# Row turns on VectorE, weight splits on ScalarE and an early gated shared expert in an adaLN block with a mixture of experts

## The chip, the core and the metric

The kernel runs on one core of a Trainium2 chip. Five engines work side by side, each through its own instructions in order: TensorE (PE; PEld is its weight load), VectorE (DVE), ScalarE (ACT), GpSimd (POOL) and SyncE (SP), which here issues nearly all DMAs. An instruction that waits holds up everything behind it on its engine. Sixteen DMA engines move the data. The metric is the device time of one execution in microseconds (us); lower is better.

## What is computed

Input x has 32 batches of 256 tokens with 128 features. The reference, cut to what matters:

```python
h = _layernorm(x) * (1 + ca) + sa
x = x + ga * _L0_attn_ref(h, ...)            # 16 heads, causal, softmax over queries
h = _layernorm(x) * (1 + cb) + sb
x = x + gb * _L0_ffn_ref(h, ...)
# the feed-forward part, for each token:
scores = sigmoid(logits);  sc = scores + gate_bias
# 2 of 4 groups of 8 experts by the sum of their two best sc; of those 16 experts the best 6
routed = einsum('te,teh->th', cw, silu(x @ w_gate) * (x @ w_up) @ w_down)
shared = silu(x @ shared_w_gate) * (x @ shared_w_up) @ shared_w_down
anchor = einsum('tl,tlh->th', acw, ao)       # one of 16 anchor experts, by the best expert
out = routed + shared + 0.1 * anchor
```

`gb` is a gate for each batch and feature. All data is 32-bit.

## The kernel before

**Attention stage** (0 to about 860 us). Tokens go in 16 chunks of 512 (`CH`), each in 8 steps of two heads. Beside the products, portions of work for other chunks (norms, routing) are dealt out by a table of steps and places. `through_dram` (L399) turns a normalized chunk: it is stored to DRAM and read back by `load_blocks` (L388) in 32x32 blocks, which DVE transposes. The turned chunk c stays in `h2_all[c]`, the residual in `x1_all[c]`. Routing writes each token's row (128 features and 52 numbers: for each of the 4 groups 8 expert weights, 4 anchor weights and the place of its result) by indirect DMA to DRAM (`rows_d`), sorted by group, twice for each token. `route_write` (L837) lays out the expert weights, even experts of a group ahead of odd ones.

**Expert stage.** 35 lists (tiles) of up to 512 rows of one group each. For tile j there are five units k: four of 128 of the group's 512 hidden columns (two experts each) and one of 128 anchor columns. A unit is, on PE, `up` (L1237): pg and pu, each a 128x128 by 128x512 product; and `down` (L1250) of the unit before: four products into py. Between them ACT makes Silu of pg (L1245) and DVE multiplies by pu (L1246) and by `bt` (L1247), the routing weights spread over the hidden columns' partitions.

The order is written out by hand. In unit 0 of tile j, SP gets `fetch_rows(j+3)` (L1159: two values loaded from a table, then one DMA of 360 KB) and `fetch_weights(j+2)` (L1175: four DMAs); in unit 1 DVE picks the tile's own group out of the rows' numbers (`weights_mine(j+2)`); in unit 2 `weights_turn(j+2)` (L1204) turns them on PE (pc), copies them by ACT (cwt), stores them to DRAM (cd) and at once reads them back spread (bt, six DMAs); in unit 3 `rows_turn(j+1)` (L1228) turns the rows by four PE transposes (ph) and an ACT copy (h). After a tile, `send` (L1273) copies py by ACT (y) and POOL writes it to `y_d` by four indirect DMAs, each row to its token's place.

**Shared expert.** For pairs n of chunks, seven ahead of the tiles and the last among them: `shared_up` (L1292) and, one step later, `shared_down` (L1305), whose result takes the place of `h2_all[c]`, copied by ACT for one chunk and by DVE for the other. The two PSUM banks that it uses in the opening are single, so the next `shared_down` waits for those copies. Emitted ahead of all this on SP are `fetch_rows` of tiles 0 to 2 and `fetch_weights` of tiles 0 and 1 (L1371 to L1374).

**The output pass.** When a chunk's tokens are complete (from tile 17 on, at most one chunk a tile, in unit 4), `pass_load` (L1328) reads both results of each token and the gate; `pass_sum` (L1345), due in unit 3 of the next tile, adds them and the shared result on DVE and multiplies by the gate on POOL; `pass_out` (L1366), due in unit 1 of the tile after, adds the residual and stores. The last chunk goes through `pass_rest` (L1354) at the end.

Of the kernel before, what the change touches and what calls it, by code (L numbers as in the profile page):

```python
# [16 lines left out]
P = 128  # L17
# [39 lines left out]
def adaln_block_kernel(  # L57
# [80 lines left out]
    def late_loads():  # L138

        nc.sync.dma_start(out=wd_sb, in_=w_down.rearrange("(k p) m -> p k m", p=P))  # L140
        nc.sync.dma_start(out=ad_sb, in_=an_down.rearrange("(k p) m -> p k m", p=P))
        nc.sync.dma_start(out=sg_sb, in_=sh_gate)
        nc.sync.dma_start(out=su_sb, in_=sh_up)
        for h in range(P // SI):
            nc.sync.dma_start(out=sd_sb[h * SI : (h + 1) * SI], in_=sh_down)
# [174 lines left out]
    with ExitStack() as actx:  # L320
# [516 lines left out]
        def route_write(c):  # L837

            w, ws, one = (chunk[c].pop(k) for k in ("w", "ws", "one"))
            meta = chunk[c]["rows"][:, :, D:].rearrange("p i (g w) -> p i g w", w=GW)  # L840
            wk = w.rearrange("p i (g k q) -> p i g k q", g=NG, q=2)
            for q in range(2):
                nc.gpsimd.tensor_tensor(
                    meta[:, :, :, q * EPG // 2 : (q + 1) * EPG // 2], wk[:, :, :, :, q],
                    ws.unsqueeze(2).unsqueeze(3).to_broadcast([P, NT, NG, EPG // 2]), ALU.mult,
                )
            pair = one.rearrange("p t (g l e) -> p t g l e", g=NG, e=2)
            nc.gpsimd.tensor_tensor(
                meta[:, :, :, EPG : GW - 1], pair[:, :, :, :, 0], pair[:, :, :, :, 1], ALU.add
            )  # L850
# [298 lines left out]
        fin = actx.enter_context(tc.tile_pool(name="fin", bufs=3, reuse_waits="tile"))  # L1149
# [9 lines left out]
        def fetch_rows(j):  # L1159
            t = T[j]  # L1160
            of, n = t["of"]
            t["g_sp"] = nc.sync.value_load(of.table[0:1, 0, n : n + 1], min_val=0, max_val=NG - 1)
            r = nc.sync.value_load(of.table[0:1, 1, n : n + 1], min_val=0, max_val=NG * SPAN)
            t["rw"] = rwp.tile([P, NT, ROW], F32, tag="rw", name=f"rw_{j}")
            got = nc.sync.dma_start(
                out=t["rw"],
                in_=rows_d[bass.ds(r, CH), :].rearrange("(p i) f -> p i f", i=NT),
            )
            if j < FIRST:
                tc.declare_no_dep(  # L1170
                    got.ins, group="late rows", reason="this tile holds rows of earlier chunks"
                )
                tc.add_to_no_dep_group("first tiles", got.ins)

        def fetch_weights(j):  # L1175
            t = T[j]
            g = t.pop("g_sp")
            for key, src, srca in (("wg", w_gate, an_gate), ("wu", w_up, an_up)):
                w = wp.tile([P, KU + 1, P], F32, tag=key, name=f"{key}_{j}")
                nc.sync.dma_start(  # L1180
                    out=w[:, 0:KU, :].rearrange("p k f -> p (k f)"),
                    in_=src[:, bass.ds(g * (KU * P), KU * P)],
                )
                nc.sync.dma_start(out=w[:, KU, :], in_=srca[:, bass.ds(g * P, P)])
                t[key] = w

        def weights_mine(j):

            t = T[j]
            of, n = t["of"]  # L1190
            mm = mp.tile([P, NT, NG, GW], F32, tag="mm", name=f"mm_{j}", bufs=1)
            nc.vector.tensor_tensor(
                mm,
                t["rw"][:, :, D:].rearrange("p i (g w) -> p i g w", w=GW),
                of.mine[:, n, :].unsqueeze(1).unsqueeze(3).to_broadcast([P, NT, NG, GW]),
                ALU.mult,
            )
            m = mp.tile([P, GW, NT], F32, tag="m", name=f"m_{j}")
            nc.vector.tensor_reduce(m, mm.rearrange("p i g w -> p w i g"), AX.X, ALU.add)
            ix = mp.tile([P, NT], U32, tag="ix", name=f"iy_{j}", bufs=5)  # L1200
            nc.vector.tensor_copy(ix, m[:, GW - 1, :])
            t.update(m=m, ix=ix)

        def weights_turn(j):  # L1204
# [10 lines left out]
            bt = bcp.tile([P, KU + 1, CH], F32, tag="bt", name=f"bt_{j}")  # L1215
            for q in range(2):
                nc.sync.dma_start(
                    out=bt[q * EI : (q + 1) * EI, 0:KU, :],
                    in_=cd[q * KU : (q + 1) * KU].partition_broadcast(EI),
                )  # L1220
            for q in range(NG):
                nc.sync.dma_start(
                    out=bt[q * LI : (q + 1) * LI, KU, :],
                    in_=cd[2 * KU + q].partition_broadcast(LI),
                )
            t["bt"] = bt

        def rows_turn(j):  # L1228
            t = T[j]
            rw = t.pop("rw")  # L1230
            ph = ps_mm.tile([P, CH], F32, tag="mm", name=f"ph_{j}")
            for i in range(NT):
                nc.tensor.transpose(ph[:, i * P : (i + 1) * P], rw[:, i, 0:D], ident)  # L1233
            t["h"] = mp.tile([P, CH], F32, tag="h", name=f"h_{j}", bufs=2)
            nc.scalar.copy(t["h"], ph)  # L1235

        def up(j, k):  # L1237
# [4 lines left out]
            nc.tensor.matmul(pg, t["wg"][:, k, :], t["h"], start=True, stop=True)  # L1242
            nc.tensor.matmul(pu, t["wu"][:, k, :], t["h"], start=True, stop=True)  # L1243
# [3 lines left out]
            nc.vector.tensor_mul(a, a, t["bt"][:, k, :])  # L1247
# [42 lines left out]


        def shared_up(n):  # L1292
# [10 lines left out]
            return n, a  # L1303

        def shared_down(n, a, banks):  # L1305
# [5 lines left out]
            for i in range(NT):  # L1311
                for h in range(2):
# [6 lines left out]
                    )  # L1319
            for h, c in enumerate(cs):  # L1320
                (nc.scalar.copy, nc.vector.tensor_copy)[h](
                    h2_all[c], py[h].rearrange("p i d -> p (i d)")
                )
# [4 lines left out]
        def pass_load(c):  # L1328
            t = S_[c]
            t["s"] = [  # L1330
                xin.tile([P, NT, D], F32, tag="xt", name=f"s{k}_{c}") for k in range(2)
            ]
            for k, s in enumerate(t["s"]):
# [5 lines left out]
            t["gate"] = fin.tile([P, BPC, D], F32, tag="gate", name=f"gate_{c}")  # L1339
            nc.sync.dma_start(  # L1340
                out=t["gate"],
                in_=gate_dram[c * BPC : (c + 1) * BPC].partition_broadcast(P),
            )

        def pass_sum(c):  # L1345
            s0, s1 = S_[c]["s"]
            nc.vector.tensor_add(s0, s0, s1)
            nc.vector.tensor_add(s0, s0, h2_all[c].rearrange("p (i d) -> p i d", d=D))
            for b in range(BPC):
                nc.gpsimd.tensor_tensor(  # L1350
# [3 lines left out]
        def pass_rest(c, b):  # L1354
# [4 lines left out]
            nc.vector.tensor_add(  # L1359
                s0, s0, h2_all[c].rearrange("p (i d) -> p i d", d=D)[:, part]  # L1360
            )
# [17 lines left out]
        for n in range(PAIRS):  # L1379
# [12 lines left out]
            if n == 3:  # L1392
                weights_turn(1)
            if n == 4:
                rows_turn(0)
        shared_down(*prev, two_banks)
# [6 lines left out]
        for j in range(LISTS):  # L1403
            for k in range(KU + 1):
# [12 lines left out]
                if k == 2 and j + 2 < LISTS:  # L1417
                    weights_turn(j + 2)
                if k == 3 and j + 1 < LISTS:
                    rows_turn(j + 1)  # L1420

# [10 lines left out]
                elif len(pair) > 1:  # L1432
                    shared_down(*pair, ((ps_mm, "mm"), (ps_mm, "mm")))
                    pair = (PAIRS,)
# [3 lines left out]
                if k == 4 and started < NCH and complete[started] <= j:  # L1438
                    pass_load(started)
                    due[j + 1, 3] = lambda c=started: pass_sum(c)  # L1440
                    due[j + 2, 1] = lambda c=started: pass_out(c)
# [61 lines left out]
```

## Time and profile before

| what | value |
|---|---|
| median of 13 executions | 1420.9 us (1416.81 to 1423.55) |
| the profiled execution | 1416.6 us, its span 1414.8 us |
| granted TensorE clock, mean | 0.986 |
| attention stage, 0 to 830: PE / DVE / ACT / POOL busy | 816 / 646 / 611 / 538 us |
| 1000 to 1200: PE / DVE / ACT / POOL busy | 200 / 123 / 64 / 59 us |
| 1200 to 1300: DMA engines' share, GB/s | 0.87, 249 |
| first product of tile 0, last y copy | 894.4, 1395.25 us |

Times in the views count from the start of the span. A line of the timeline has start, duration, engine, source line, operation, output and inputs, how many instructions were merged, and in brackets the idle time before it and what ended it. "SPq" is an issue of a DMA on SP's queue, not its landing. A busy time of PE is modelled from pipelined products, so the distance between starts tells more than durations.

### The profile page before, as it was taken

Reading aid. Unit: us, or ns where it says so; the run is one execution under the profiler, and the core shown is the slowest. Engines: PE = TensorE matmul, PEld = TensorE weight load, DVE = VectorE, ACT = ScalarE, POOL = GpSimd, SP = SyncE. Lnnn points to the kernel's source line nnn. Section 1 sums busy time; section 2 is a strip of 40 time slices with the busy share of each in tenths; the row PEclk is TensorE's granted clock in tenths of the full one; section 3 lists DMA queues with packets and bytes.
Section 4 is the critical chain, followed back from the end, with each engine's and each line's share of the span. In section 5 each row is a group of like instructions: output and inputs, shape, how many; then the busy total and the mean of one; then the engine's idle time right before and its main releaser. Section 6 shows DMA issues by size and latency. Waiting matters only on the chain. (4 is left out here: it accounts for less than half of the span.)

```text
span 1414.8 us, 33682 instructions
## 1 busy us (share of the span) xinstructions
PE 1356.8 (96%) x10543; PEld 841.9 (60%) x10543; DVE 1016.2 (72%) x4277; ACT 797.3 (56%) x2767; POOL 762.1 (54%) x1294
## 2 busy tenths in 40 slices
PE   7999999999999999999999997889999999999994
PEld 2566666666666666566666663555666666656662
DVE  5666888888878778888777775666665567766664
ACT  4777777777777777777777773322333333332331
POOL 3536467767767866767866645444232233434333
PEclk9999999999999999999999999999999999999997
DMA  4773622022022022022122114767667777878782
GB/s 152 276 265 108 219 74 60 32 74 61 31 74 62 31 73 62 30 74 62 38 68 50 39 35 128 185 165 191 171 184 211 186 217 221 256 233 245 233 221 61
DMA packets 183599, 182.50 MB, mean 129 GB/s; under 512 B 81520, under 2 KB 142656, under 8 KB 178944
## 3 DMA queue, kind: packets, MB, share of 16 engines
q1 hardware_dynamic: 172112, 159.62, 40.8%
q0 software_dynamic: 10624, 20.21, 4.3%
q8 instruction: 86, 1.41, 0.4%
q14 instruction: 89, 0.73, 0.2%
q10 hardware_dynamic: 688, 0.53, 0.1%
HBM read 121.37 MB, written 59.70 MB: 128 GB/s over the span
## 5 line engine op out<-in xcount | busy, mean ns | idle before, releaser
L549 ACT ACTIVATE e<-e,mn 128x256 f32<-128x256 f32 (+1 forms) x1024 | 453.5, 445 | 200.6 <-DVE mn L539 158.8
L539 DVE CUSTOM_DVE_ANT_0 e<-psc,mask 128x256 f32<-128x256 f32 (+1 forms) x1024 | 306.5, 345 | 9.7 <-PE pav L586 3.3
L568 POOL TENSOR_TENSOR vs<-v,rc 128x256 f32<-128x256 f32 x256 | 151.2, 611 | 223.8 <-DVE rc L557 214.8
L1279 POOL DMA_INDIRECT y_d<-y,iy x140 | 137.7, 984 | 239.9 <-ACT y L1276 207.7
L518 PEld LDWEIGHTS psc<-q,k 64*128 64x128 f32 x2048 | 166.2, 187 | 113.4 <-issue 101.6
L1246 DVE TENSOR_TENSOR a<-a,pu 128x512 f32<-128x512 f32 x175 | 120.0, 686 | 153.9 <-PE pu L1243 107.3
L1245 ACT ACTIVATE a<-pg 128x512 f32<-128x512 f32 x175 | 104.4, 597 | 178.1 <-PE pg L1242 123.4
L518 PE MATMUL psc<-q,k 64*128 64x256 f32 (+1 forms) x2048 | 202.1, 336 | 0.0
L586 PE MATMUL pav<-e,vs 128*64 128x256 f32 (+1 forms) x2048 | 194.7, 332 | 6.1 <-POOL vs L568 6.1
L549 ACT ACTIVATION_READ_ACCUMULATOR e<-e,mn 128x1 f32 x1024 | 192.4, 188 | 0.0
L1268 PEld LDWEIGHTS py<-wd_sb,a 128*128 128x128 f32 x1120 | 146.5, 191 | 71.9 <-issue 54.3
L1242 PE MATMUL pg<-h,wg 128*128 128x512 f32 x350 | 181.7, 601 | 1.4 <-ACT h L1235 1.4
L1243 PE MATMUL pu<-h,wu 128*128 128x512 f32 x350 | 180.0, 596 | 0.0
L468 PEld LDWEIGHTS po<-wo_sb,z 128*64 128x64 f32 x2048 | 120.4, 137 | 70.3 <-issue 69.6
L586 PEld LDWEIGHTS pav<-e,vs 128*64 128x64 f32 x2048 | 126.8, 136 | 58.8 <-POOL vs L568 6.7
L479 DVE TENSOR_TENSOR v<-pv,bv_sb 128x512 f32<-128x512 f32 x128 | 88.3, 690 | 92.8 <-PE pv L468 63.8
L1268 PE MATMUL py<-wd_sb,a 128*128 x1120 | 148.1, 275 | 2.9 <-issue 1.5
L856 POOL DMA_INDIRECT rows_d<-rows,ix x128 | 129.9, 1015 | 37.4 <-issue 34.6
L489 DVE TENSOR_SCALAR q<-pq,negbq 128x512 f32<-128x512 f32 x128 | 95.9, 749 | 64.2 <-PE pq L468 62.5
L468 PE MATMUL pv<-wqkv_sb,n_t 128*64 128x512 f32 x512 | 132.8, 598 | 2.3 <-DVE q L489 1.6
L468 PE MATMUL pq<-n_t,wqkv_sb 128*64 128x512 f32 x512 | 133.5, 600 | 0.7 <-ACT n_t L302 0.7
L468 PE MATMUL po<-wo_sb,z 128*64 128x128 f32 x2048 | 133.6, 273 | 0.0
(239 smaller groups left out, 1771.6 us busy)
## 6 DMA issues: line engine op xcount, KB each, us to landing
bt<-cd SPq DMA_DIRECT2D x70, 512.0 KB
rows_d<-blank SPq DMA_DIRECT2D x69, 360.0 KB
rw<-rows_d SPq DMA_DIRECT2D x35, 360.0 KB
wg<-in_w_gate_dram SPq DMA_DIRECT2D x35, 256.0 KB
wu<-in_w_up_dram SPq DMA_DIRECT2D x35, 256.0 KB
bt<-cd SPq DMA_DIRECT2D x140, 64.0 KB
s<-y_d SPq DMA_DIRECT2D x32, 256.0 KB
mb<-mod_dram SPq DMA_DIRECT2D x31, 256.0 KB
```

The lines of the kernel that those rows point to most:

```text
L468: nc.tensor.matmul(ps[r], a[:, r], b, start=start, stop=stop)
L518: nc.tensor.matmul(pb[h][:, cols], k[r, o + kb * P : o + (kb + 1) * P], q[r, o + kb * P : o + S], start=True, stop=True,)
L539: nc.vector.tensor_tensor_reduce(e[:, cols], ps[:, cols], mask[:, cols], 1.0, 3e38, ALU.add, ALU.min, mn[:, b, kb, h : h + 1],)
L549: nc.scalar.activation(e[:, cols], e[:, cols], AF.Exp, bias=mn[:, b, kb, h : h + 1], scale=-1.0, accum_out=sm[:, b, kb, h : h + 1],)
L568: nc.gpsimd.tensor_tensor(vs[:, 2 * b : 2 * b + 2], vt[:, 2 * b : 2 * b + 2, col : col + P].rearrange("p k (h d) -> p k h d", h=2), rc[:, ...
L586: nc.tensor.matmul(pav[h * DH : (h + 1) * DH, o + kb * P : o + S], vs[:, 2 * b + kb, h, :], e[:, 0 : 2 * P] if kb == 0 else e[:, 2 * P : 3 ...
L856: sent = nc.gpsimd.indirect_dma_start(out=rows_d[:, :], out_offset=bass.IndirectOffsetOnAxis(ap=ix[:, k, i : i + 1], axis=0), in_=rows[:, ...
L1242: nc.tensor.matmul(pg, t["wg"][:, k, :], t["h"], start=True, stop=True)
L1243: nc.tensor.matmul(pu, t["wu"][:, k, :], t["h"], start=True, stop=True)
L1246: nc.vector.tensor_mul(a, a, pu)
L1268: nc.tensor.matmul(t["py"][:, i, :], a[:, i * P : (i + 1) * P], w, start=k == 0 and i == 0, stop=k == KU and i == NT - 1,)
L1279: sent = nc.gpsimd.indirect_dma_start(out=y_d[:, :], out_offset=bass.IndirectOffsetOnAxis(ap=ix[:, i : i + 1], axis=0), in_=y[:, i, :], in ...
```

## The change

1. Rows. `fetch_rows` loads the 52 numbers (`rw`) and the features (`rh`) apart; the features come in 32x32 blocks by four DMAs of `load_blocks`, and `rows_turn` becomes one DVE transpose. The four PE transposes and the ACT copy go.
2. Hidden columns. Unit k now takes every fourth hidden column of the group from k on, so that partition p belongs to expert p // 16 in all four units: `bt` has two planes in place of five and takes one DMA of 256 KB for the experts (and four for the anchors, as before). `w_down` is loaded in that order. The gate and up weights arrive in their old order (`raw`) and ACT copies them to the new one: `split_weights(j+1)`, wg in unit 2, wu in unit 3, behind what was there. `route_write` needs one POOL product in place of two.
3. The spread of the weights is a function of its own, `weights_spread`, called in unit 4, two units behind the store.
4. Shared expert. `shared_up` also loads the gates of both chunks. `shared_down` multiplies by them on DVE (four products a pair, no copies) and POOL adds the result to the residual.
5. Output pass. `pass_sum` is one sum, due in unit 0 of the second tile after the load; the gate is multiplied on DVE in unit 2 (`pass_gate`), the residual added in unit 4. `pass_rest` loses a sum. The tiles of the pass come from pools of their own (6 for s, 5 for gates).

```diff
@@ late_loads
-        nc.sync.dma_start(out=wd_sb, in_=w_down.rearrange("(k p) m -> p k m", p=P))
+        nc.sync.dma_start(
+            out=wd_sb.rearrange("p (g k) m -> p g k m", g=NG),
+            in_=w_down.rearrange("(g p k) m -> p g k m", g=NG, p=P),
+        )
@@ fetch_rows
-            t["rw"] = rwp.tile([P, NT, ROW], F32, tag="rw", name=f"rw_{j}")
...
+            t["rw"] = rwp.tile([P, NT, ROW - D], F32, tag="rw", name=f"rw_{j}")
+            t["rh"] = rwp.tile([P, CH // BLK, BLK], F32, tag="rh", name=f"rh_{j}")
+            rows = rows_d[bass.ds(r, CH), :]
+            got = [
+                nc.sync.dma_start(
+                    out=t["rw"], in_=rows[:, D:].rearrange("(i p) f -> p i f", p=P)
+                ),
+                *load_blocks(t["rh"], rows),
+            ]
@@ fetch_weights
-                w = wp.tile([P, KU + 1, P], F32, tag=key, name=f"{key}_{j}")
+                raw = wp.tile([P, P, KU], F32, tag=f"{key}r", name=f"{key}r_{j}")
...
+        def split_weights(j, key):
+
+            t = T[j]
+            raw, a = t[key]
+            w = wp.tile([P, KU, P], F32, tag=key, name=f"{key}_{j}", bufs=2)
+            nc.scalar.copy(w, raw.rearrange("p f k -> p k f"))
+            t[key] = [w[:, k, :] for k in range(KU)] + [a]
@@ weights_turn
-            bt = bcp.tile([P, KU + 1, CH], F32, tag="bt", name=f"bt_{j}")
-            for q in range(2):
-                nc.sync.dma_start(
-                    out=bt[q * EI : (q + 1) * EI, 0:KU, :],
-                    in_=cd[q * KU : (q + 1) * KU].partition_broadcast(EI),
-                )
...
+        def weights_spread(j):
+
+            t = T[j]
+            cd = t.pop("cd")
+            bt = bcp.tile([P, 2, CH], F32, tag="bt", name=f"bt_{j}")
+            nc.sync.dma_start(
+                out=bt[:, 0, :], in_=cd[0:EPG].unsqueeze(1).to_broadcast([EPG, P // EPG, CH])
+            )
...
@@ rows_turn
-            ph = ps_mm.tile([P, CH], F32, tag="mm", name=f"ph_{j}")
-            for i in range(NT):
-                nc.tensor.transpose(ph[:, i * P : (i + 1) * P], rw[:, i, 0:D], ident)
...
-            nc.scalar.copy(t["h"], ph)
+            nc.vector.transpose(t["h"], t.pop("rh").rearrange("p x r -> p (x r)"))
@@ shared_up, shared_down
-            return n, a
+            return n, a, [load_gate(c) for c in cs]
...
-                (nc.scalar.copy, nc.vector.tensor_copy)[h](
-                    h2_all[c], py[h].rearrange("p i d -> p (i d)")
-                )
+                o = h2_all[c].rearrange("p (i d) -> p i d", d=D)
+                for b in range(BPC):
+                    nc.vector.tensor_tensor(
+                        tokens(o)[:, b], tokens(py[h])[:, b], by_batch(gates[h])[:, b], ALU.mult
+                    )
+                nc.gpsimd.tensor_tensor(x1_all[c], x1_all[c], o, ALU.add)
@@ the opening: pairs n
                 weights_turn(1)
+                weights_spread(0)
             if n == 4:
+                weights_spread(1)
                 rows_turn(0)
+            if n == 5:
+                split_weights(0, "wg")
+                split_weights(0, "wu")
@@ the tiles
+                if k in (2, 3) and j + 1 < LISTS:
+                    split_weights(j + 1, ("wg", "wu")[k - 2])
                 if k == 3 and j + 1 < LISTS:
                     rows_turn(j + 1)
+                if k == 4 and j + 2 < LISTS:
+                    weights_spread(j + 2)
...
                     pass_load(started)
-                    due[j + 1, 3] = lambda c=started: pass_sum(c)
-                    due[j + 2, 1] = lambda c=started: pass_out(c)
+                    due[j + 2, 0] = lambda c=started: pass_sum(c)
+                    due[j + 2, 2] = lambda c=started: pass_gate(c)
+                    due[j + 2, 4] = lambda c=started: pass_out(c)
```

## The prediction

> **What bounds the kernel now.** I read the page's busy line first, then busy time by stage, then PE's timeline in one tile of the expert stage, then SP's.
>
> ```profile
> PE 1356.8 (96%) x10543; PEld 841.9 (60%) x10543; DVE 1016.2 (72%) x4277; ACT 797.3 (56%) x2767; POOL 762.1 (54%) x1294
> ```
>
> PE is the engine to follow. The change leaves the attention stage (0 to 860) almost alone, so its worth is read from the opening of the expert stage (862 to 894, the shared expert), the 35 tiles (894 to 1395) and the tail. One tile on PE:
>
> ```profile
> 1134.51 1.05 PE L1268 MATMUL py<-wd_sb,a 128*128 x8
> 1135.40 1.02 PE L1242 MATMUL pg<-h,wg 128*128 128x512 f32 x2
> ...
> 1139.84 1.05 PE L1268 MATMUL py<-wd_sb,a 128*128 x8
> 1140.73 0.60 PE L1233 MATMUL ph<-ident,rw 128*128 128x128 f32 x4
> 1141.17 1.02 PE L1242 MATMUL pg<-h,wg 128*128 128x512 f32 x2
> ```
>
> No idle time stands on these rows. From py to the next pg it is 0.89 us (1134.51 to 1135.40), and with the four row turns between 1.33 (1139.84 to 1141.17): the turns cost PE 0.44 a tile. A unit is 2.61 (pg 0.87, pu 0.85, py 0.89), a tile 5 x 2.61 + 0.11 (pc) + 0.44 = 13.60; the y copies (L1276) indeed start 13.60 apart from 1024 to 1242. Tiles 1 to 7 need 13.5 us more than that in all, tiles after 1242 some 5.2 more. SP's queue shows the late loss:
>
> ```profile
> 1281.66 0.42 SPq L1214 DMA_DIRECT2D cd<-cwt  x1
> 1285.08 1.27 SPq L1217 DMA_DIRECT2D bt<-cd  x2
> 1286.72 1.72 SPq L1222 DMA_DIRECT2D bt<-cd  x4
> ...
> 1293.63 0.35 SPq L1165 DMA_DIRECT2D rw<-rows_d  x1
> ...
> 1296.78 0.45 SPq L1214 DMA_DIRECT2D cd<-cwt  x1
> ```
>
> Once output chunks are also loaded and stored, SP needs 14.4 us a tile (cd to cd: 13.4 to 15.4 from 1167 on), more than PE's 13.6. It falls behind about 0.8 a tile until the s loads come too late for pass_sum (L1347: 9.9 us of waiting for them). The opening:
>
> ```profile
> 866.49 6.17 SPq L1165 DMA_DIRECT2D rw<-rows_d  x3
> 872.73 0.66 SPq L1180 DMA_DIRECT2D wg<-in_w_gate_dram  x1
> ...
> 878.84 0.37 SPq L1214 DMA_DIRECT2D cd<-cwt  x1
> ```
>
> ```profile
> 875.51 0.68 DVE L1321 COPY h<-sy 128x512 f32<-128x512 f32 x1
> ```
>
> ```profile
> 875.50:885.00 9.50, 8.80 (x56) 4.13 (x58) 9.12 (x38) 3.13 (x7) 1.21 (x2) 0.82 0.63 181
> 885.00:894.40 9.40, 8.73 (x91) 5.25 (x87) 8.32 (x39) 3.68 (x8) 6.61 (x21) 1.00 0.76 167
> ```
>
> In the windows the columns are PE, PEld, DVE, ACT, POOL. DVE is busy 17.4 of 18.9 us there: the opening is bound by DVE and PE together, and DVE starts on shared results at 875.5, while SP is still issuing loads until 878.8.
>
> **The change part by part.** The sum is made against the profiled execution: 1414.8 span, 1416.6 with what lies around it. The median of 13 runs is 1420.9, 4.3 above that one.
>
> *Turns from PE to DVE.* PE loses 0.44 in 34 tiles: **-15.0**. DVE gains one 128x512 transpose, 0.70 (rows L456 and L652). In a unit DVE has two products of 0.69 (1.38 of 2.61), and extras now go one to a unit: sum 0.69, mine 1.20, gate 2 x 0.40 to 0.43, turn 0.70, out 0.68. The fullest unit is 2.58 of 2.61, and a product is done 0.5 us before PE loads it (1133.59 against 1134.09), so I cost them at nothing; with that cover gone each late one would cost its excess over 0.5. ACT loses the h copy (0.585).
>
> *Splits by ACT.* Two copies of 128x512 a tile. No row shows ACT reading at a stride. Bounds: 0.585 (L1235, contiguous) and 1.4 times that, 0.82, from DVE's strided reduce against its contiguous product of the same 208 columns (L1199 513 ns, L1192 368). I take 0.6, since a copy is nearest to a copy. ACT sits idle 2.0 us a unit, so mostly this costs nothing. But in unit 2 a split queues behind cwt, which waits for PE's pc, and Silu of the next unit waits behind both. In 23 tiles cwt starts within 1.1 us of pc, in 12 it starts 1.6 to 3.1 after. There Silu would come 1.2 late (1.4 with 0.82), of which 0.27 is hidden behind pu and 0.5 by the slack above: 0.5 to 0.7 for each of up to 12. Between 0 and 8.6 I take **+3**. The Trainium skill ("SBUF — State Buffer", Door 1: The DMA port swizzle) says SBUF has 16-byte lines and every access that crosses to a new line pays; here each element is 16 bytes from the last. By that rule the splits would stand at the slow end, the term would be 8.6 and the time 1431.6; no row here shows it on ACT.
>
> *Row loads and bt.* One 360 KB load of rows becomes one of 208-byte pieces and four of 128-byte pieces; bt falls from two of 512 KB to one of 256 KB. The same block loads (hb, 236.8 to 242) kept the 16 DMA engines 49% busy for 5.2 us, 512 packets of hd among them: about 2 us for 2048 small packets. Against that, 768 KB of bt go, 3.4 us at the 220 GB/s that bt moved at 1143 to 1146. DMA (share 0.87 at 1200 to 1300) gets lighter.
>
> On SP, each row load is about 0.55 (four hb in 1.96, plus 0.07 for the address): +2.2 a tile, less 0.6 for a bt.
>
> *Spread two units later.* Between the cd store (unit 2) and the spread (unit 4) nothing else is queued on SP. In the tiles SP still waits at bt for cd to land (70.9 us over 32 waits, 2.2 each): I cost this at **0**.
>
> *Late stage.* SP's cycle: 14.4 + 2.2 - 0.6 - 1.5 (waits of rw, weights and gate for slow bt loads, 20 us in all over the stage) = 14.5, against 13.16 on PE. It falls behind 1.3 a chunk tile instead of 0.8. pass_sum now comes two units later, so the s loads may be 11.3 late instead of 6.4: 8.5 chunk tiles instead of 7.5. So the late loss stays near what it was, 5 chunk tiles x 1.3 = 6.5 against 5.2: **+1** (-5 to +8).
>
> *Opening.* The gates of the first pair are emitted behind three row fetches and two weight fetches. SP leaves those at 878.8; twelve more loads of 0.55 make 885.4, and 2 us landing (cd to bt: 2.1) 887.4, against 875.5 for DVE's first copy. That is 12; 8 if SP is spared the slow stretch 868 to 874 (some 4 us). I take **+11**. Every instruction behind that gate on DVE waits, and PE for its banks. Then DVE has 7 x (4 x 0.396, L628, - 0.689, L1321) + 0.7 = **+7**. POOL gets 14 sums of 128x512, 1.4 each (twice 0.72, L1350), in front of chunk 15's normalization; its rows leave later, SP waits for them at hb, and the gates of the last pair are behind hb: **+3** (0 to 6). In return tile 0's own loss goes (2.9 us at 904 waiting for that same hb, 1.5 of half clock behind it; 15.5 is the bare path): **-4**, of which a new cold start takes its part. Opening: **+17** (10 to 24).
>
> *Tail.* pass_rest loses two sums of 0.424: **-0.9**. POOL's gates there go too, but the last s load waits for y_d to land.
>
> Sum: -15.0 + 3 + 1 + 17 - 0.9 = **+5.1**: 1421.7 for the profiled execution, **1426** on the scale of the median.
>
> **Rivals.**
> 1. *The opening's delay is absorbed (faster).* Tiles 1 to 7 lose 13.5 us while chunk 15 is routed and the last pair is run: PE waits for counts (1.7 at 940), for h from ACT (1.0 at 975), for a late cwt at 923. Of it PE's own work is 4.6 (pl, pr, sg, su, sy, by their rows); if the other 8.9 are waits for things that a later start meets ready, they go: 1426 - 8.9 = **1417**. It decides from 8 us absorbed (5.1 + 2.8). For it: h leaves ACT. Against: chunk 15's steps are dealt by unit and shift along.
> 2. *The spread does what it says (no change).* If SP were spared the 2.2 of waiting, its cycle is 12.3, below PE's, and the late loss goes: 5.1 - 1 - 5.2 = -1.1, **1420**. Against it: nothing is queued between.
> 3. *SP bounds the last stage (slower).* If rows cost 0.7 each and the waits stay, 15.2: 2.0 behind a chunk tile, the slack of 11.3 is gone after 5.6 of 15, the other 9 cost 2 each: 18 - 5.2 = 13 instead of 1: **1438**.
>
> **Chances.** Forecast 0.45 (1420 to 1432), rival 1 0.25, rival 2 0.12, rival 3 0.18. The range runs from rival 1 with the opening at its low end (-15 + 3 + 1 + 10 - 0.9 - 8.9 = -10.8, 1410) past rival 3 to 1442, the forecast with the opening at +24 and the splits and the late stage at their upper ends in part (7 + 5.6 + 7 = 19.6 would be 1445.6). A measurement can tell 0.2% (2.8 us) from no change. Faster 0.28 (rival 1 and the forecast's edge), within 0.12 (rival 2), slower 0.60.
>
> **What would show it.** PE: unit 2.61 and the y copies 13.16 apart in mid stage. DVE: the first gated product of the shared expert at 884 to 888 behind "DMA gate", and the first y copy near 932 (now 915.5). SP: cd to cd 14.5 in chunk tiles, bt still waiting for cd. ACT: splits of 0.6, and PE waits for DVE's product after unit 2 where cwt is late. Wrong would be: gates landing by 878, a split over 0.9 us, DVE waiting for rh.

## The result and the profile after

The changed kernel takes **1444.9 us** (median of 10; 1439.9 to 1451.7) against 1421.0 of the kernel before on the same chip: ratio **1.017** (1.0155 to 1.0184). The profiled execution has a span of 1441.7 against 1414.8, 26.9 more. The busy line of the page:

```profile
PE 1352.1 (94%) x10403; PEld 827.4 (57%) x10403; DVE 1048.8 (73%) x4349; ACT 840.7 (58%) x2794; POOL 756.9 (53%) x1264
```

PE lost its turns (140 instructions fewer), yet the span grew: its idle time did. Where, is read from four marks: the start of SP's last block loads of the attention stage (hb), the first product of tile 0, and the y copies of ACT, each a tile's end (all us, worked out from the starts in the timelines):

| stretch | before | after | difference | foretold |
|---|---|---|---|---|
| start to hb | 862.8 | 864.3 | +1.5 | 0 |
| hb to first pg | 31.6 | 55.8 | +24.2 | with the next row +17 |
| first pg to y0 | 21.1 | 20.5 | -0.6 | |
| y0 to y8 | 122.3 | 124.9 | +2.6 | the three rows of tiles -11 |
| y8 to y20 | 163.2 | 165.8 | +2.6 | |
| y20 to y34 | 194.3 | 193.4 | -0.9 | |
| y34 to the end | 19.6 | 17.1 | -2.5 | -0.9 |

The first row is no finding: over the profiled executions of all kernels here, hb lay between 858.8 and 867.8.

**The opening.** SP's and DVE's timelines of the kernel after:

```profile
868.07 0.50 SPq L1169 DMA_DIRECT2D rw<-rows_d  x1
...
883.36 0.33 SPq L1191 DMA_DIRECT2D wua<-in_an_up_dram  x1
883.73 5.27 SPq L1308 DMA_DIRECT2D gate<-gate_dram  x6
```

```profile
887.90 1.42 DVE L1347 TENSOR_TENSOR h<-sy,gate 128x256 f32<-128x256 f32 x4 [14.68 <-DMA gate<-gate_dram]
889.24 0.85 DVE L681 TENSOR_SCALAR sig<-th 128x128 f32<-128x128 f32 x1
890.01 1.77 DVE L638 TENSOR_TENSOR x<-xt,o_t 128x512 f32<-128x512 f32 x1
...
895.61 1.17 DVE L691 TENSOR_TENSOR hi<-scb 128x64 f32<-128x64 f32 x1
...
901.15 0.37 DVE L365 BATCH_NORM_AGGREGATE ln_mv<-ln_stats 128x2 f32<-128x6 f32 x4
...
901.96 1.24 DVE L701 TENSOR_TENSOR lo<-lo 128x16 f32<-128x16 f32 x1
```

The gates leave SP behind every row and weight fetch, and DVE stands 14.68 us for them. Then single operations of DVE take far longer than their neighbours: 1.17 us for one of 128x64, 1.24 for one of 128x16, where the instructions just after (L692, L702) take 0.21 and 0.17. POOL's timeline has a new operation, the sum of the shared result, beside each of them:

```profile
888.74 2.49 POOL L1350 TENSOR_TENSOR x<-x,h 128x512 f32<-128x512 f32 x2 [19.47 <-DVE h L1347]
...
894.16 2.54 POOL L1350 TENSOR_TENSOR x<-x,h 128x512 f32<-128x512 f32 x2 [1.52 <-DVE h L1347]
...
900.65 2.51 POOL L1350 TENSOR_TENSOR x<-x,h 128x512 f32<-128x512 f32 x2 [1.52 <-DVE h L1347]
```

The pairs of sums cover 888.7 to 891.2, 894.2 to 896.7 and 900.7 to 903.2, and the long DVE operations start at 889.2, 890.0, 895.6 and 902.0, all inside. Three of them end just behind a pair, whatever their own length: L638, L691 and L701 at 891.78, 896.78 and 903.20, the pairs at 891.23, 896.70 and 903.16. L365, inside the same pair as L701, takes 0.37, as it does in experiment 12 without the sums. So the long ones are held until the sum ends and not slowed in proportion; why some DVE operations are held and others not, the runs do not show. The granted clock of PE falls as well (third column from the right):

```profile
864.00:880.00 16.00, 8.86 (x76) 4.44 (x72) 2.64 (x5) 3.35 (x5) 4.06 (x5) 0.93 0.61 105
880.00:892.00 12.00, 2.70 (x16) 2.27 (x16) 4.10 (x7) 0.00 (x0) 3.10 (x3) 0.50 0.62 181
892.00:905.00 13.00, 10.74 (x56) 4.06 (x58) 12.62 (x41) 1.71 (x4) 9.17 (x10) 0.71 0.32 94
```

PE is busy 2.70 of the 12 us at 0.50. In the 13 us at 0.71 DVE is the fuller engine (12.62 against PE's 10.74). What the lower clock cost was not isolated.

**A tile.** Unit 2 of a middle tile, PE, ACT and DVE together:

```profile
1111.97 0.27 PE L1223 MATMUL pc<-ident,m 128*48 128x128 f32 x1
...
1113.68 0.26 ACT L1227 COPY cwt<-pc 48x128 f32<-48x128 f32 x1 [2.67 <-PE pg L1258]
...
1113.84 1.11 ACT L1199 COPY wg<-wgr 128x512 f32<-128x512 f32 x1
...
1114.86 0.59 ACT L1260 ACTIVATE a<-pg 128x512 f32<-128x512 f32 x1
...
1115.48 0.69 DVE L1261 TENSOR_TENSOR a<-a,pu 128x512 f32<-128x512 f32 x1 [2.72 <-ACT a L1260]
...
1116.20 0.69 DVE L1262 TENSOR_TENSOR a<-a,bt 128x512 f32<-128x512 f32 x1
...
1116.95 0.38 PE L1283 MATMUL py<-wd_sb,a 128*128 x1 [0.38 <-DVE a L1262]
```

cwt starts 1.71 after pc; the split behind it takes 1.11, not 0.6; Silu waits for it, the two products of DVE follow, and PE stands until they are done. Such a tile takes 13.8. Where cwt comes 0.35 after pc, the tiles are 13.16 apart, as foretold. In the profiled execution it is late in 23 of 35 tiles (12 before).

### The profile page after: what moved, and what is told of

Its sections match the earlier page's. It is cut to its first block, busy times and chain, and to the rows that moved or that the text cites. A ratio compares the mean times of both kernels' runs of the same rounds, so it can differ in the third digit from the quotient of the medians.

```text
span 1441.7 us, 33883 instructions
## 1 busy us (share of the span) xinstructions
PE 1352.1 (94%) x10403; PEld 827.4 (57%) x10403; DVE 1048.8 (73%) x4349; ACT 840.7 (58%) x2794; POOL 756.9 (53%) x1264
## 4 chain that ended last, share of the span: by engine, by line
PE 75%; DVE 8%; issue 5%; DMA 4%; SPq 4%; POOL 3%; ACT 1%; POOLq 0%; DVEq 0%; ACTq 0%
PE psc L521 13%; PE pav L589 12%; PE py L1283 8%; PE pv L471 8%; PE pq L471 7%; PE pk L471 7%; PE po L471 7%; PE pg L1258 7%; PE pu L1258 6%; DVE a L1261 1%; DVE a L1262 1%; SPq L395 1%; DVE e L542 1%; ACT a L1260 1%; DMA gate<-gate_dram 1%
## 5 line engine op out<-in xcount | busy, mean ns | idle before, releaser
L589 PE MATMUL pav<-e,vs 128*64 128x256 f32 (+1 forms) x2048 | 194.9, 332 | 6.1 <-POOL vs L571 6.1
L1283 PE MATMUL py<-wd_sb,a 128*128 x1120 | 151.1, 278 | 23.5 <-DVE a L1262 19.3
L1258 PE MATMUL pg<-h,wg 128*128 128x512 f32 x280 | 144.7, 599 | 0.0
L1258 PE MATMUL pu<-h,wu 128*128 128x512 f32 x280 | 143.7, 595 | 0.0
```

The lines of the kernel that those rows point to most:

```text
L589: nc.tensor.matmul(pav[h * DH : (h + 1) * DH, o + kb * P : o + S], vs[:, 2 * b + kb, h, :], e[:, 0 : 2 * P] if kb == 0 else e[:, 2 * P : 3 ...
L1258: nc.tensor.matmul(ps, t[key][k], t["h"], start=True, stop=True)
L1283: nc.tensor.matmul(t["py"][:, i, :], a[:, i * P : (i + 1) * P], w, start=k == 0 and i == 0, stop=k == KU and i == NT - 1,)
```

## The experiments

The edits are made in the changed kernel unless another is named. Ratios are to the kernel before on the same chip, with 95% intervals; the kernel after stands at 1.017. "Opening" is hb to the first pg (before 31.6, after 55.8), "middle" y8 to y20 (163.2, 165.8), "late" y20 to y34 (194.3, 193.4).

**1. e1, gates first.** The first four gates leave SP ahead of the fetches.

```diff
-            return n, a, [load_gate(c) for c in cs]
+            return n, a, [first_gates.pop(c, None) or load_gate(c) for c in cs]
...
+        first_gates = {c: load_gate(c) for c in range(4)}
         for j in range(3):
             fetch_rows(j)
```

> The gates of the first two pairs are loaded ahead of the row and weight fetches; all else is as in the changed kernel (1444.85 us). Theory (the gates wait their turn on SP): DVE's first gated product starts at about 876 instead of 887.9, 12 us go, about 1433. Rival (DVE and POOL work bounds the opening and the wait only overlaps it): tile 0's first product moves by less than 4, 1441 or more. A small loss is expected by both, since four gate loads of 0.4 us now stand ahead of the row fetches.

Measured 1429.8, ratio 1.0076 (1.0046 to 1.0106); opening 45.5. The gates' place cost 10.3 us of the opening; the theory held (DVE's first gated product starts at 872.2, earlier than foretold).

**2. e2, splits later.** `split_weights(j + 1)` in units 3 and 4, not 2 and 3: it no longer stands behind cwt.

```diff
-                if k in (2, 3) and j + 1 < LISTS:
+                if k in (3, 4) and j + 1 < LISTS:
```

> The two splits of a tile stand in units 3 and 4 instead of 2 and 3, so that no split is queued between cwt and Silu. Theory (a split of 1.12 us behind a late cwt holds back Silu): tiles are 13.16 apart from the 8th on instead of 13.80, about 20 tiles gain 0.64, 13 us, about 1432. Rival (the turn on DVE or the row loads cost the 0.64): tiles stay at 13.8, 1445. A gain smaller than 13 at 13.16 a tile would mean that SP takes over earlier in the late stage.

1432.8, ratio 1.0087 (1.0059 to 1.0115). Middle 157.9, twelve tiles of 13.16; PE's waits for DVE's product fell from 20.4 to 6.4 us in all. Held. In ten of the twelve middle tiles cwt is late as before, but now Silu follows it at once, and the tile takes 13.16 all the same:

```profile
1095.96 0.26 ACT L1227 COPY cwt<-pc 48x128 f32<-48x128 f32 x1 [2.55 <-PE pg L1258]
1096.12 0.59 ACT L1260 ACTIVATE a<-pg 128x512 f32<-128x512 f32 x1
```

**3. e3, contiguous split.** The same copy without the stride.

```diff
-            nc.scalar.copy(w, raw.rearrange("p f k -> p k f"))
+            nc.scalar.copy(w.rearrange("p k f -> p (k f)"), raw.rearrange("p f k -> p (f k)"))
```

> The splits read the weights in the order in which they lie, so the columns of gate and up weights come out in the wrong order (part of the computation is changed); places and sizes are the same. Theory (reading one element in each 16 bytes makes the copy take 1.118 us): a split takes 0.59, Silu behind a late cwt is 0.5 late beyond its slack at most, tiles are 13.2 to 13.35 apart, about 1434 to 1437. Rival (the copy is long because of its size or of what runs beside it): it stays at 1.1 and the time at 1445.

1435.8, ratio 1.0108 (1.0076 to 1.014); middle 158.9. On ACT's timeline the copy behind a late cwt now takes 0.62:

```profile
1121.68 0.26 ACT L1227 COPY cwt<-pc 48x128 f32<-48x128 f32 x1 [2.58 <-PE pg L1258]
1121.84 0.62 ACT L1199 COPY wg<-wgr 128x512 f32<-128x512 f32 x1
```

Only the order of reading differs, so the stride of 16 bytes is what makes it 1.11. Held.

**4. e4, spread at the store.** `weights_spread` back in unit 2.

```diff
                     weights_turn(j + 2)
+                    weights_spread(j + 2)
-                if k == 4 and j + 2 < LISTS:
-                    weights_spread(j + 2)
```

> The spread stands in unit 2 again, right behind the store. Theory (nothing else is queued on SP between the two, so the place makes no difference in the tiles): the same time within 2 us, 1445, with the same waits of SP for cd. Rival (the two units hide the store's landing): SP waits more for cd, its cycle grows by up to 2.2 a tile, the late stage loses 10 or more, 1455.

1439.1, ratio 1.013 (1.0106 to 1.0154): no slower than after, even 0.4% faster, where the same time was foretold. SP's waits for cd grow from 47.1 to 58.0 us, and the late stage by 1.5 (194.9); the middle is 1.4 shorter, and cwt is late in 17 tiles of the run, not 23. The later place alone gains nothing in the time.

**5. e5, turns alone.** The kernel before with only the rows' loads in blocks and their turn on DVE.

```diff
+                *load_blocks(t["rh"], rows),
...
-                nc.tensor.transpose(ph[:, i * P : (i + 1) * P], rw[:, i, 0:D], ident)
...
-            nc.scalar.copy(t["h"], ph)
+            nc.vector.transpose(t["h"], t.pop("rh").rearrange("p x r -> p (x r)"))
```

> The kernel before with one part of the change alone: rows loaded in blocks and turned on DVE. Theory (PE gains 0.44 a tile, and SP then bounds the late stage, since four more loads cost it 2.2 a tile and bt is still large): tiles 13.16 apart in mid stage, -15; in the chunk tiles SP needs 16.6 a tile, falls behind 3.4 a tile, its slack of 6.4 is gone after two, the other 13 cost up to 3.4 each instead of 5 in all: +15 to +39, together 1421 to 1445, with the y copies more than 15 apart there. Rival (SP has room): 1406, y copies 13.2 apart to the end.

1463.5, ratio 1.0299 (1.0277 to 1.0321): the direction of the SP theory, but far more than either theory gave. Tiles are 13.16 apart until the output pass begins; then they lose: middle 178.8, late 220.8, SP waits 86.9 us for cd, `pass_sum` 40.5 for its loads. Four more loads a tile beside the large bt cost far more than PE saves. That SP's issues are the limit, and not the transfers, and that the smaller bt pays for the loads in the change, is argued and not shown.

**6. e6, host order.** Gate and up weights stored in DRAM in the split order; no splits.

```diff
+        "w_gate": get("ffn_w_gate").transpose(1, 0, 2).reshape(D, NG, P, -1).transpose(0, 1, 3, 2).reshape(D, E * EI),
...
-                if k in (2, 3) and j + 1 < LISTS:
-                    split_weights(j + 1, ("wg", "wu")[k - 2])
```

> The changed kernel without its splits: the gate and up weights lie in DRAM in the order of the split columns from the start, so ACT copies nothing (an order of data outside the timed program). Theory: as with the splits in units 3 and 4, tiles of 13.16 from the 8th on until SP bounds them, 1430 to 1433. Rival (what the splits cost is mostly ACT's and DMA's time, not the wait behind cwt): clearly faster than with the splits moved, 1425 or less.

1442.9, ratio 1.0149 (1.0129 to 1.017). Missed. Middle 157.9, as without the splits' stall; but late 198.7, and in the profiled execution hb was 3.6 later than after. Why the late stage lost 5 is not settled; e18, with the tiles of after, has 197.4 there, so part of it may be scatter between executions.

**7. e7, sums later.** POOL's sums one a tile in tiles 1 to 14, not in the opening.

```diff
-                nc.gpsimd.tensor_tensor(x1_all[c], x1_all[c], o, ALU.add)
+                if n == PAIRS:
+                    nc.gpsimd.tensor_tensor(x1_all[c], x1_all[c], o, ALU.add)
...
+                if k == 3 and 1 <= j <= 2 * PAIRS:
+                    c = j - 1
+                    nc.gpsimd.tensor_tensor(
+                        x1_all[c], x1_all[c],
+                        h2_all[c].rearrange("p (i d) -> p i d", d=D), ALU.add,
+                    )
```

> POOL adds the gated shared results to the residual one chunk a tile in tiles 1 to 14 instead of in the opening. In the changed kernel's opening DVE's small products run 0.6 to 1.1 us long while POOL adds (6.0 us over what the same instructions take in the kernel before), and POOL's queue holds up chunk 15's rows. Theory (both cost the opening): tile 0's first product comes 6 to 10 us earlier, 1435 to 1439. Rival (the wait for the first gates hides them): within 3 us, 1442 or more.

1444.7, ratio 1.0161 (1.0134 to 1.0189). Missed: opening 49.3 (-6.5), but y0 to y8 128.0 (+3.1) and late 197.6 (+4.3), though no moved sum stands in the late stage. Moved, the sums gained nothing.

**8. e8, shared as before.** Shared expert as in the kernel before (copies, added in `pass_sum`, no early gates, no POOL sums); all else as after.

```diff
...
-                o = h2_all[c].rearrange("p (i d) -> p i d", d=D)
-                for b in range(BPC):
-                    nc.vector.tensor_tensor(
-                        tokens(o)[:, b], tokens(py[h])[:, b], by_batch(gates[h])[:, b], ALU.mult
-                    )
-                nc.gpsimd.tensor_tensor(x1_all[c], x1_all[c], o, ALU.add)
+                (nc.scalar.copy, nc.vector.tensor_copy)[h](
+                    h2_all[c], py[h].rearrange("p i d -> p (i d)")
+                )
...
+            nc.vector.tensor_add(s0, s0, h2_all[c].rearrange("p (i d) -> p i d", d=D))
...
```

> The changed kernel with the shared expert as in the kernel before (copies by ACT and DVE, no gates in the opening, no sums on POOL; the shared result is added in pass_sum, one sum more a chunk). Theory (the opening's 25 us are the gates, their products and the sums): the first y copy comes at 918 to 922 instead of 940.6, tiles behind it as in the changed kernel, 1421 to 1426. Rival (the row fetches on SP delay the opening by themselves): 1432 or more.

1423.4, ratio 1.0012 (0.9993 to 1.0031); opening 32.2. The time held (the first y copy came at 912.0, earlier than foretold): net, the whole loss is the shared expert's part; the rest of the change comes to nothing.

**9. e9: e8 with splits in units 3 and 4.**

> The changed kernel with the shared expert as before (copies, added in pass_sum, no early gates, no POOL sums) and the splits in units 3 and 4. My theory: what is left of the loss in the tiles is the split behind the late cwt; without it the tiles from 9 to 20, 13.8 apart with the splits in units 2 and 3, come 13.16 apart: about 12 x 0.64 = 7.7, a few more of the early ones, less what SP takes back late: 1412 (1408 to 1417). The rival, that the late stage is bound by SP alone and takes back all that the middle wins: 1420 to 1424, no change against 1423.4.

1407.6, ratio **0.993** (0.9909 to 0.995). Faster than both kernels. The theory held: by the ratio 1411 on the scale of e8, as foretold. Middle 157.9, late 193.3, where e8 has 165.8 and 196.9: the late stage took nothing back.

**10. e10: e9 with one DMA for the anchors' plane of bt.**

```diff
-            for q in range(NG):
-                nc.sync.dma_start(
-                    out=bt[q * LI : (q + 1) * LI, 1, :],
-                    in_=cd[EPG + q].partition_broadcast(LI),
-                )
+            nc.sync.dma_start(
+                out=bt[:, 1, :],
+                in_=cd[EPG : EPG + NG].unsqueeze(1).to_broadcast([NG, P // NG, CH]),
+            )
```

> The kernel of the run before, with the anchors' plane of bt spread by one DMA in place of four (the same bytes). Four issues take SP 1.80 us, one of that shape 0.68. Theory: SP's issues bound the late tiles (cd to cd 14.2 to 15.4), so 1.1 less a tile over some 12 to 15 tiles from number 20 on: about 12 less than the run before, 1400 (1396 to 1406). Rival one: the late stage is bound by the landing of the s and cd transfers, not by issues: within 2 of the run before. Rival two: one DMA of 128 partitions lands later than four of 32, bt late: slower than the run before.

1421.4, ratio 1.0026 (1.0009 to 1.0042); late 207.4. The theory failed and the second rival's forecast came: SP issues less, but the same bytes move slower. The windows some 2 to 4 us behind the spread's first issue, of e9 and then of e10 (last columns: share of the DMA engines, GB/s):

```profile
1113.00:1114.00 1.00, 1.00 (x6) 0.65 (x6) 0.96 (x2) 0.33 (x1) 0.00 (x0) 1.00 0.54 207
1114.00:1115.00 1.00, 1.00 (x4) 0.40 (x3) 0.06 (x1) 0.60 (x1) 0.00 (x0) 1.00 0.79 256
```

```profile
1123.00:1124.00 1.00, 1.00 (x6) 0.59 (x5) 0.96 (x2) 0.28 (x1) 0.00 (x0) 1.00 0.51 186
1124.00:1125.00 1.00, 1.00 (x4) 0.46 (x3) 0.00 (x0) 0.60 (x1) 0.00 (x0) 1.00 0.32 92
```

With one DMA the engines' share falls to 0.32 while the transfer is still out, and from 1150 on the issues of a tile's four row loads behind it take SP 3.58 to 5.50 us, where they took 1.69 to 2.57. That fewer engines carry it is argued from the share, not shown.

**11. e11, three mends.** The changed kernel with e1, e2 and e10's edit.

> The changed kernel, all of its parts kept, with three places changed: the gates of pairs 0 and 1 ahead of the row and weight fetches, the splits in units 3 and 4, the anchors' plane of bt by one DMA. If the causes are separate, 1444.9 - 15.1 (gates) - 12.1 (splits) - some 10 (issues) = 1408 (1402 to 1414). If the gains overlap (the late stage meets SP earlier when the start is earlier), 1415 to 1422.

1438.0, ratio 1.0134 (1.0111 to 1.0156); late 207.9. Missed for e10's reason; experiment 15 has the two good mends alone.

**12. e12, no sums.**

```diff
-                nc.gpsimd.tensor_tensor(x1_all[c], x1_all[c], o, ALU.add)
```

> The changed kernel without POOL's 16 sums of the gated shared result into the residual: the shared expert's share is left out of the output. Theory: the sums on POOL hold up DVE and POOL's own routing steps in the opening; without them the first y copy comes some 7 us earlier, as when they were spread over the tiles, and nothing is given back: 1437 (1434 to 1440). Rival: the opening is bound by the gates and the DVE products, and the sums lie beside them: 1443 to 1446.

1428.9, ratio 1.0085 (1.0066 to 1.0104); opening 48.8, 7.0 less. The same DVE operations as above, with no sum beside them:

```profile
886.87 0.21 DVE L681 TENSOR_SCALAR sig<-th 128x128 f32<-128x128 f32 x1
887.00 0.68 DVE L638 TENSOR_TENSOR x<-xt,o_t 128x512 f32<-128x512 f32 x1
...
890.87 0.22 DVE L691 TENSOR_TENSOR hi<-scb 128x64 f32<-128x64 f32 x1
...
895.84 0.17 DVE L701 TENSOR_TENSOR lo<-lo 128x16 f32<-128x16 f32 x1
```

0.85, 1.77, 1.17 and 1.24 became 0.21, 0.68, 0.22 and 0.17. With L687 (0.93 and 0.28) and L699 (0.52 and 0.14) the six operations that start beside the first three pairs of sums were 4.8 us longer: POOL's sums hold up what DVE does beside them. By the ratio the time fell by 12 where 7 were foretold. In the profiled execution the first eight intervals are 4 shorter and hb is 4 earlier, so 7.0, of the opening alone, is the figure to keep.

**13. e13: e9 with the output pass's loads on ACT's queue,** in unit 1 of the next tile, for chunks 0 to 11.

```diff
-                    pass_load(started)
+                    if started < 12:
+                        due[j + 1, 1] = lambda c=started: pass_load(c, nc.scalar)
+                    else:
+                        pass_load(started)
```

> The fastest kernel so far (shared expert as before, splits in units 3 and 4) with the output pass's three loads of a chunk (two s and the gate, chunks 0 to 11) issued by ACT's queue, in unit 1 of the next tile, in place of SP's. Theory, SP's issues bound the late tiles: SP's cycle falls by some 1.8 (3 issues) from 14.5 to about 12.7, below PE's 13.16, and the 14 last intervals take 185 to 188 in place of 193.3: ratio to before 0.988 (0.986 to 0.990), against 0.993. Rival, the transfers bound them: within 0.002 of 0.993. Rival, three issues on ACT hold up Silu: over 0.995.

1460.1, ratio 1.0358 (1.033 to 1.0386). No test of SP: The third forecast came, over 0.995: ACT stood some 7 to 8 us at the loads before the next Silu, 89.0 us in all over 12 times. They now come after the next `send`, so they may wait for its rows as well; the trace names no releaser. SP's question stayed open.

**14. e14: e1 and e12 together.**

> The changed kernel with the gates of pairs 0 and 1 first and without POOL's sums (the shared share is left out of the output). If the terms of the opening add: from the last block load to the first product 55.8 - 10.3 - 7.0 = 38.5 (37 to 40), against 31.6 before, the rest being DVE's products in place of copies (foretold as 7); time about 1444.9 - 15.1 - 12 = 1418, ratio 0.998. If the two hide one another: 41 to 45.

1407.1, ratio 0.9982 (0.9966 to 0.9998); opening 40.9, just outside the band for terms that add. DVE waits 6.80 us for the third pair's gates, still behind the fetches; experiment 18 asks whether that makes the rest. Its time is helped by a middle of 157.9 (cwt was never late here), which is not the edit's doing.

**15. e15: e1 and e2 together,** all parts of the change kept.

> The changed kernel, all of its parts kept, with gates of pairs 0 and 1 first and splits in units 3 and 4. If the two terms add: 1.017 - 0.0094 - 0.0083 = 0.9993 (0.997 to 1.002), no change against before. If the late stage takes back: 1.003 to 1.008.

1413.5, ratio 1.0025 (1.001 to 1.004). Between the two bands: opening and splits nearly add, and the change is then still no gain. Since cwt was never late in this run either, its middle of 157.9 says nothing of the splits' place; e2 does.

**16. e16: e9 with `fetch_weights(j + 2)` in unit 3,** between store and spread on SP.

```diff
-                if k == 0 and j + 2 < LISTS:
-                    fetch_weights(j + 2)
...
+                if k == 3 and j + 2 < LISTS:
+                    fetch_weights(j + 2)
```

> The fastest kernel so far (shared expert as before, splits in units 3 and 4) with fetch_weights(j+2) moved from unit 0 to unit 3, so that on SP its four loads stand between the cd store and the spread. The same transfers, the same queue. Theory: the spread two units later gained nothing because nothing stood between store and spread on SP; now the 2.2 of waiting for cd are filled by 2.3 of issues, SP's cycle falls from 14.5 to about 12.3, below PE's 13.16, and the last 14 intervals take 185 to 188 in place of 193.3: ratio to before 0.988 (0.986 to 0.990) against 0.993 without it; waits of SP for cd under 15 us in all (56 without it). Rival, the transfers bound the late tiles: the waits for cd go and the last 14 intervals stay at 191 to 195, ratio within 0.002 of 0.993.

1393.7, ratio **0.983** (0.981 to 0.985): the fastest, and more than the theory's 0.988. SP's queue in the kernel after, then in e16:

```profile
1211.40 0.38 SPq L1229 DMA_DIRECT2D cd<-cwt  x1
1214.40 0.67 SPq L1237 DMA_DIRECT2D bt<-cd  x1
```

```profile
1210.68 0.43 SPq L1229 DMA_DIRECT2D cd<-cwt  x1
1211.31 0.35 SPq L1186 DMA_DIRECT2D wgr<-in_w_gate_dram  x1
...
1213.04 0.33 SPq L1191 DMA_DIRECT2D wua<-in_an_up_dram  x1
1213.47 0.68 SPq L1237 DMA_DIRECT2D bt<-cd  x1
```

The gap of 2.6 between store and spread is filled with the four loads. SP's waits for cd, in e9 and in e16 (us in total, times, longest):

```profile
SPq L1237 <- DMA cd<-cwt: 56.2, 28, 3.6
```

```profile
SPq L1237 <- DMA cd<-cwt: 2.5, 1, 2.5
```

Late 183.3, all tiles but the last two at 13.16; PE is busy 100.00 of the 100 us from 1200, and the same transfers go through at 209 GB/s there, where e9 had 189. So SP's cycle bound e9's late stage, not the transfers.

**17. e17: e15 with the same move,** all parts of the change kept.

> The changed kernel, all of its parts kept, with gates of pairs 0 and 1 first, splits in units 3 and 4 and fetch_weights in unit 3. By the same theory 5 to 7 less than the run with the first two mends (ratio 1.0025): 0.998 (0.996 to 1.000). By the rival: 1.001 to 1.004.

1411.6, ratio 0.9956 (0.9941 to 0.9972). The theory held, with a little more than foretold. Late 183.3 again; against e16 the shared part still costs 1.3%.

**18. e18: e14 with six gates first** (and a sixth buffer).

```diff
+        first_gates = {c: load_gate(c) for c in range(6)}
```

> The changed kernel without POOL's sums (the shared share is left out of the output) and with the gates of the first three pairs, six in place of four, ahead of the row and weight fetches (and a sixth gate buffer). If the gate wait makes the rest: the third pair's wait of 6.8 goes, two more issues ahead of the fetches cost 0.9, and from the last block load to the first product it is about 35 (33.5 to 36.5) against 40.9 and 31.6 before; time 5 to 6 less, ratio 0.994. If DVE's products make it, as foretold (7): 39 to 41, ratio 0.997 to 0.999.

1431.1, ratio 1.0043 (1.0028 to 1.0057); opening 41.8, no shorter. Missed: the third pair's wait went, the fourth pair's came (3.35, 1.10 and 0.54 us for later gates). Six gates ahead push the fetches and the rest of the gates back; that the queue as a whole is the limit is argued, not shown, since 41.8 also lies close to the band of the other account, DVE's products (39 to 41). The time is not comparable with e14's, since cwt was late in this middle (166.0). The products' own share of the opening stays open.

## Why the prediction was wrong

The direction was right, the time just outside the range. The sum was +5.1; the profiled executions differ by +26.9. The 21.8 between them are three steps that failed by about as much each, the splits by 8, the opening by 8 and the turns with the late stage by 7, less 1.6 of the tail. The prediction had upper ends of 8.6, +24 and +8 for the splits, the opening and the late stage, and by its own sum 1445.6 for these together; that is nearly what came, and its range ended at 1442.

- **Splits: +3 foretold, about +11 measured: the first step that failed.** Two things were wrong in one term. The copy takes 1.11 and not 0.6, outside the bounds 0.585 to 0.82: the upper one came from a DVE reduction with another stride. And cwt was late in 23 tiles, not 12. e2 against after gives 7.9 in the twelve middle intervals, 3.2 in the first eight and none later (by the ratios 12 in all). The 3.2 are less sure: e1, whose tiles are those of after, is 5.0 shorter in the first eight. The price of a late tile, 0.5 to 0.7 foretold and 0.64 measured, was right by luck. With a copy of the assumed length (e3, 0.62) the ten late tiles of the middle cost 0.9 in all, 0.09 each: the forecast gave the wait too little cover and the copy too little length. Its own subtraction (1.2 and 1.4, less 0.27 and 0.5) also gives 0.43 to 0.63 a tile, so 7.6 for twelve and not 8.6. The Trainium skill ("SBUF — State Buffer", Door 1: The DMA port swizzle) says that each access that crosses to a new 16-byte line pays a penalty; this case agrees, with 1.11 us where each element is 16 bytes from the last and 0.61 to 0.62 contiguous.
- **Opening: +17 foretold, +25.1 measured** at the first y copy, 1.5 of it ahead of hb. The gates' place was right: 887.4 foretold for DVE's first gated product, 887.90 measured; +11 foretold, 10.3 taken back by e1. The step that failed is POOL's sums: priced +3 as a delay of POOL's own queue, they cost 7.0 (e12), since they also hold up DVE, 4.8 us in six operations. That tile 0 would get back 4 failed too (0.6). The products' +7 was not isolated: on DVE they take 1.41 against 0.69, 5.1 for seven pairs.
- **Turns: -15.0 foretold.** Exactly so in the middle: without the splits' stall 163.15 becomes 157.91, -5.24 for twelve tiles, 0.44 each. In the late stage only 0.9 came, where -6.2 + 1 was foretold: SP bounds it, so what PE saves there shows nowhere. Its loss over PE's own pace, 5.2 before, is 10.1 after (193.4 against the 183.3 of e16), and the forecast had 6.2. The forecast's sum does not close here: of the 15 chunk tiles that rival 3 counts, 8.5 within the slack leave 6.5 and not 5, a loss of 8.5 at 1.3 each and not of 6.5. In the first eight intervals e2 has -0.7, not -3.5; what took the rest was not followed up.
- **Spread two units later: 0 foretold,** and e4 agrees in that the earlier place is not slower. The reason given, nothing queued between, is supported by e16: with the loads between, 10 us come in the late stage.
- **Tail: -0.9 foretold, -2.5 measured;** not followed up.
- **The rivals.** The opening was not absorbed (y0 to y8 grew by 2.6). The spread did not do what it says; e16, which fills its gap, gains 10.0 where this rival had priced the late loss at 6.2. That SP bounds the last stage came in part: a loss of 10.1, between the forecast's 6.2 and this rival's 18.

Still open: why cwt sometimes starts 0.35 and sometimes 1.6 to 1.7 after pc with the same code around it; what the products and the lower clock alone cost in the opening; e6's late stage.

## What to carry to other kernels

An operation put behind a late one in an engine's queue costs what the slack behind it does not cover (here 0.09 us a tile for a copy of 0.62 and 0.64 for one of 1.11), so its price must be known in the access pattern it will have: a row of another engine with another stride is no bound. Moving an issue later gained nothing here while nothing else of the same queue stood in the gap: what helped was other work between store and load. An engine that gets work "beside" another's may hold up that other's instructions without any wait in the trace: compare the durations of the same lines. And when several terms have upper ends, a range should allow for all of them at once, or say why not.

## What the runs showed of the hardware

- ACT's copy of 128x512 f32 took 1.11 us reading at a stride of 16 bytes and 0.61 to 0.62 contiguously.
- Beside POOL's two-input sums of 128x512, DVE operations of 0.17 to 0.22 us took 0.85 to 1.24, and one of 0.68 took 1.77; they ended 0.03 to 0.55 us behind a sum. A BATCH_NORM_AGGREGATE beside the same sums kept its length.
- The same 256 KB spread by one DMA from four rows of DRAM moved at a lower share of the DMA engines (0.32 against 0.79 in the same place) than by four DMAs, and later issues on that queue took 3.58 to 5.50 us for four loads instead of 1.69 to 2.57.
- In the opening the granted clock was 0.93 over 16 us in which PE was busy 8.86, 0.50 over the next 12 (busy 2.70) and 0.71 over the 13 behind them (busy 10.74).
